# A transformer decoder in f32: the second feed-forward layer in 49 sub-products, with weight sums formed once and streamed

## The chip, the cores and the metric

The kernel runs on one core of a Trainium2 chip. Times are microseconds of device time for one execution. The core has a matrix engine (TensorE, PE in the profile; its weight loads are listed apart as PEld), VectorE (DVE), ScalarE (ACT), GpSimd (POOL), and SyncE (SP), from whose queue this kernel issues all of its DMA transfers. Every engine works through its own instructions in order. Matmul results go to PSUM, eight banks of 128 partitions x 512 f32 values; VectorE and ScalarE read them from there, and here GpSimd works on SBUF only. "Granted clock" is the share of full speed that TensorE's throttle allowed.

## The reference

An encoder layer over a short context (2 x 77 tokens), then a decoder layer over 2 x 2048 tokens of width 512, with 16 heads of width 32, all in f32. The change concerns the last step, the decoder's feed-forward:

```python
yn = _ln(y, dec_n1_s, dec_n1_b)
y = y + _mha(yn, yn, dec_sa_in_w, dec_sa_in_b, dec_sa_out_w, dec_sa_out_b, sb)     # causal
y = y + _mha(_ln(y, dec_n2_s, dec_n2_b), memory, dec_ca_in_w, dec_ca_in_b, dec_ca_out_w, dec_ca_out_b, cb)
h = _ln(y, dec_n3_s, dec_n3_b)
y = y + (jax.nn.relu(h @ dec_ff1_w.T + dec_ff1_b) @ dec_ff2_w.T + dec_ff2_b)       # 512 -> 2048 -> 512
```

## The kernel before

**Stages.** Tokens are handled in 8 blocks of 512 (`blocks`, four for each of the two sequences). First comes self-attention, in 128 *units* (block x 4 groups of heads x 4 token tiles of 128). A list of jobs is written out for every unit: `jobs` (projections), `light`, `ahead` and `late` (small work before and after them), run by `slot(n)`. The encoder is laid into the units of the first block, and the first block's cross-attention into the first units of the second sequence. The probabilities of two successive units lie at the two ends of one large buffer, `pp`; for a sequence's third block (units 32 to 47 and 96 to 111) they leave 4096 columns free in its middle, and parts of `vv` and `kT` are free then too.

**The feed-forward stage** follows, and with it the cross-attention of block x + 1 is interleaved with the feed-forward of block x. A block has 56 *slots*, 28 for each layer (L1100). In the last loop (L1350) a slot takes one step of `cross(x + 1)` and then `ff_slot`. `cross` (L1225) has a plan by slots: normalisation `n2` in slots 0 to 7, query projections in 9 to 12, and then for each token tile, seven slots apart from slot 14, score (+0), exp (+2), sums and normalisation (+3), transposes (+6), times V (+9), output product (+11) and the normalisation `n3` (+13, +15, +17). Cross-attention uses PSUM banks 0 to 3, the feed-forward 4 to 7.

**Two-by-two products.** Each of the two matrix products of the feed-forward is split into 2 x 2 quarters and done with seven products of quarters in place of eight (Strassen's scheme: `PARTS`, L1083, lists for each product the sum of left quarters, the sum of right quarters, and the result quarters to which it is added or from which it is taken). Layer 1: a product has four slots n of 4 matmuls, each with 128 x 128 weights and 256 tokens moving. Layer 2: likewise, with 128 x 128 pieces of h as weights and 256 output columns moving; the four slots of a product add up in PSUM. An f32 matmul is two records in the profile, a load and a multiplication each.

**Where the sums come from.** `prepare(s + 3)` (L1137) forms the operands of the slot three ahead, through L1148: sums of weight quarters and of n on GpSimd, sums of h quarters on VectorE. Both weight matrices lie in `pp` (`w_1`, `w_2`, loaded at L1053 and L1349), so that a sum of weights is formed anew in each of the 8 blocks. The results of every product are read out by themselves: in `first_product` ScalarE copies the first contribution to a quarter of h (L1178, L1176 with the sign turned), VectorE adds the later ones (L1180), and ScalarE applies the bias and relu after the last one (L1183). In `second_product` VectorE adds each result to the y in SBUF, at L1202, once or twice a product; y already holds the residual. Finished rows of y are stored at L1207, and the y of block x + 2 is loaded into the same place at L1209; two blocks of y are held.

**Queues.** All transfers stand in SP's one queue in program order, and a transfer that has to wait holds up those behind it. GpSimd's queue holds the sums of L1148, the row additions L750, the small powers L743 and the normalisation L804 of cross-attention.

Of the kernel before, what the change touches and what calls it, by code (L numbers as in the profile page):

```python
# [17 lines left out]
P = 128  # L18
B, T, S, D = 2, 2048, 77, 512
H, HD, DFF = 16, 32, 2048  # L20
NC = D // P
# [33 lines left out]
def tile_encoder_decoder(ctx: ExitStack, tc: tile.TileContext, ins, out):  # L55
# [102 lines left out]
    with (  # L158
# [751 lines left out]
        ahead = {n: [] for n in range(-1, len(units) + NU)}  # L910

# [83 lines left out]
        late = {n: [] for n in light}  # L995
# [21 lines left out]
        for r, fs in first_cross().items():  # L1017
# [3 lines left out]
        w_1 = pp[:, : END // 2].rearrange("p (c o) -> p c o", c=NC)  # L1021
        w_2 = pp[:, END // 2 :].rearrange("p (f o) -> p f o", f=NF)
        hT = kT.rearrange("p c (f n) -> p (c f) n", n=MB)
        vflat = vv.rearrange("p a d -> p (a d)")
        nT2 = vflat[:, 12 * D :].rearrange("p (c n) -> p c n", n=MB)
        pr = oT_all.rearrange("p a q -> p (a q)")[:, : H * S]
# [3 lines left out]
        ys = [  # L1030
            vflat[:, i * TB * D : (i + 1) * TB * D].rearrange("p (t d) -> p t d", t=TB) for i in range(2)
        ]

        first_ring = []

        def y_of(x, t):
            return ys[x % 2][:, t, :]
# [12 lines left out]

        def w_1_load(i):

            nc.sync.dma_start(w_1[:, :, ts(i, D)], wchunk("dec_ff1_wT", i * D))  # L1053
# [11 lines left out]
        def late_loads():  # L1065
# [12 lines left out]

        TOK = MB // 2
        PARTS = {  # L1083

            1: (((1, 1), "+", (2, 2)), ((1, 1), "+", (2, 2)), (("+", 1, 1), ("+", 2, 2))),
            2: (((2, 1), "+", (2, 2)), ((1, 1),), (("+", 2, 1), ("-", 2, 2))),
            3: (((1, 1),), ((1, 2), "-", (2, 2)), (("+", 1, 2), ("+", 2, 2))),
            4: (((2, 2),), ((2, 1), "-", (1, 1)), (("+", 1, 1), ("+", 2, 1))),
            5: (((1, 1), "+", (1, 2)), ((2, 2),), (("-", 1, 1), ("+", 1, 2))),
            6: (((2, 1), "-", (1, 1)), ((1, 1), "+", (1, 2)), (("+", 2, 2),)),  # L1090
            7: (((1, 2), "-", (2, 2)), ((2, 1), "+", (2, 2)), (("+", 1, 1),)),
        }
        ORDER = {1: (1, 4, 5, 7, 2, 3, 6), 2: (3, 5, 1, 4, 7, 2, 6)}

        def order_of(x, layer):

            return ORDER[layer if x else 2]

        SIGN = {"+": ALU.add, "-": ALU.subtract}
        slots = [  # L1100
            (x, layer, i, n)
            for x in range(len(blocks))
            for layer in (1, 2)
            for i in order_of(x, layer)
            for n in range(4)
        ]
        w_ring = [vflat[:, (8 + i) * D : (9 + i) * D].rearrange("p (c o) -> p c o", c=2) for i in range(4)]
        h_ring = [vflat[:, (12 + i) * D : (13 + i) * D].rearrange("p (c o) -> p c o", c=2) for i in range(4)]
        oflat = oT_all.rearrange("p a q -> p (a q)")
        n_ring = [  # L1110
            oflat[:, H * S + i * D : H * S + (i + 1) * D].rearrange("p (c o) -> p c o", c=2) for i in range(2)
        ]
        xt_ring = [pts_all[:, 7, :]]
        per = len(slots) // len(blocks)
        turns = {"w": 0, "h": 0, "n": 0, "xt": 0}
        operands, ff_banks = {}, {}

        def in_ring(name, ring):
            turns[name] += 1
            return ring[turns[name] % len(ring)]  # L1120

        def quarter_w1(a, c, n):
            o = (a - 1) * (DFF // 2) + n * 2 * P
            return w_1[:, 2 * c - 2 : 2 * c, o : o + 2 * P]

        def quarter_n(a, c, n):
            return nTt[:, 2 * a - 2 : 2 * a, ts(c - 1, TOK)]

        def quarter_h(a, c, n):
            f = (c - 1) * (NF // 2) + 2 * n  # L1130
            return hT[:, f : f + 2, ts(a - 1, TOK)]

        def quarter_w2(a, c, n):
            f = (a - 1) * (NF // 2) + 2 * n
            return w_2[:, f : f + 2, ts(c - 1, D // 2)]

        def prepare(s):  # L1137

            if s >= len(slots):
                return  # L1140
            x, layer, i, n = slots[s]
            early = s < 12

            def operand(parts, quarter, name, ring, engine):
                if len(parts) == 1:
                    return quarter(*parts[0], n)
                dst = in_ring(name, ring)
                engine.tensor_tensor(dst, quarter(*parts[0], n), quarter(*parts[2], n), SIGN[parts[1]])  # L1148
                return dst

            pa, pb, _ = PARTS[i]
            if layer == 1:
                b = operand(pb, quarter_n, "n", first_ring if early else n_ring, nc.gpsimd) if n == 0 else operands[s - 1][1]
                operands[s] = operand(pa, quarter_w1, "w", w_ring, nc.gpsimd), b
            else:
                b = operand(pb, quarter_w2, "w", w_ring, nc.gpsimd)
                operands[s] = operand(pa, quarter_h, "h", h_ring, nc.vector), b

        def first_product(s):
            x, layer, i, n = slots[s]  # L1160
            a, b = operands[s]
            mm = ff_bank()
            for f in range(2):
                for c in range(2):
                    nc.tensor.matmul(  # L1165
                        mm[:, ts(f, TOK)], a[:, c, ts(f, P)], b[:, c, :], start=(c == 0), stop=(c == 1)
                    )
            order = order_of(x, 1)
            got = mm.rearrange("p (f n) -> p f n", f=2)
            for sign, r, c in PARTS[i][2]:  # L1170
                users = [j for j in order if (r, c) in [u[1:] for u in PARTS[j][2]]]
                f = (r - 1) * (NF // 2) + 2 * n
                dst = hT[:, f : f + 2, ts(c - 1, TOK)]
                if i == users[0]:
                    if sign == "-":
                        nc.scalar.activation(dst, got, AF.Identity, scale=-1.0)  # L1176
                    else:
                        nc.scalar.copy(dst, got)  # L1178
                else:
                    nc.vector.tensor_tensor(dst, dst, got, SIGN[sign])  # L1180
                if i == users[-1]:
                    for e in range(2):
                        nc.scalar.activation(dst[:, e, :], dst[:, e, :], AF.Relu, bias=vec("dec_ff1_b", f + e))  # L1183

        def second_product(s):
            x, layer, i, n = slots[s]
            b, m = blocks[x]
            lhs, rhs = operands[s]
            if n == 0:
                ff_banks[x] = ff_pair()  # L1190
            mm = ff_banks[x]
            for c in range(2):
                for t in range(2):
                    nc.tensor.matmul(  # L1194
                        mm[:, t, :], lhs[:, c, ts(t, P)], rhs[:, c, :],
                        start=(n == 0 and c == 0), stop=(n == 3 and c == 1),
                    )
            if n < 3:
                return
# [194 lines left out]
```

## Time and profile before

| what | value |
|---|---|
| median of 3 runs (lowest to highest) | 2893.01 us (2889.47 to 2893.07) |
| the profiled execution: its time, its span | 2889.82 us, 2888.0 us |
| granted clock, mean | 0.992 |
| feed-forward stage, first matmul to end | 1756.8 to 2888.0 us |
| one block in that stage (the 2nd, 3rd, 5th, 6th and 7th) | 144.5 us |
| the 4th block, beside which the next sequence's bias tables are added | 148.4 us |
| the last block, without cross-attention | 101.3 us |
| PE idle in the 4th block; in each of the other later ones before the last | 3.1 us; below 0.1 us |
| DVE, ACT, POOL busy in a 144.5 us block | 90.6, 45.6, 83.8 us |
| DMA traffic over the span | 137 MB, 48 GB/s |
| DMA traffic from 1750 us on | 27 MB, 24 GB/s |

How to read it: the stage between 1756.8 us and the end is where the change works; an engine's busy time against the length of a block says how near it is to setting the pace. The busy share of PE counts a matmul from its start to its modelled end; the distance between starts is the pace.

### The profile page before, as it was taken

The page shows a single profiled execution, that of the slowest core. Times are in us where ns is not written, and L with a number is a line of the kernel's source. Part 1 is how long each engine was busy: PE and PEld are TensorE (multiplying, and loading weights), DVE is VectorE, ACT ScalarE, POOL GpSimd, SP SyncE. Part 2 cuts the span into 40 slices and gives each one's busy share as a digit, 9 for nine tenths or more (in the row PEclk, how much of TensorE's full clock was granted, in tenths as well). Part 3 has the DMA queues.
Part 4 walks back from the last instruction along what each step waited for, and adds up shares of the span by engine and source line. Part 5 has one row for each costly group of instructions (what it writes and reads, how often), then busy time and mean ns, then how long its engine had stood idle before and what let it go on. Part 6 is the DMA issues. An engine that isn't in the chain of part 4 may idle for free.

```text
span 2888.0 us, 60347 instructions
## 1 busy us (share of the span) xinstructions
PE 2852.6 (99%) x24438; PEld 2021.1 (70%) x24438; DVE 2048.3 (71%) x5566; ACT 1299.5 (45%) x2431; POOL 746.3 (26%) x605
## 2 busy tenths in 40 slices
PE   9899999999999999999999999999999999999999
PEld 5557666666666556666666677777777777777788
DVE  4667688878986678788778894757575757575745
ACT  3344465556665446565556674323232323232321
POOL 0100000000000101000000004465656474747464
PEclk9899999999999999999999999999999999999999
DMA  6413301201112502211201115000002000000000
GB/s 174 114 32 122 108 16 56 64 16 45 35 42 63 140 20 74 74 31 49 56 16 38 42 31 193 18 30 1 30 1 48 1 30 1 30 1 30 1 15 15
DMA packets 118456, 137.34 MB, mean 48 GB/s; under 512 B 18544, under 2 KB 73888, under 8 KB 118050
## 3 DMA queue, kind: packets, MB, share of 16 engines
q1 hardware_dynamic: 118178, 133.49, 16.0%
q8 instruction: 192, 3.15, 0.5%
q14 instruction: 86, 0.70, 0.1%
HBM read 111.59 MB, written 21.86 MB: 46 GB/s over the span
## 4 chain that ended last, share of the span: by engine, by line
PE 93%; DVE 4%; ACT 1%; DMA 1%; issue 1%; SPq 0%; POOL 0%; DVEq 0%; ACTq 0%; POOLq 0%
PE psum L425 17%; PE psum L1194 14%; PE psum L1165 13%; PE psum L371 11%; PE psum L442 8%; PE psum L830 4%; PE psum L765 4%; PE psum L239 4%; PE psum L251 4%; PE psum L215 4%; PE psum L226 3%; PE psum L810 2%; PE psum L780 1%; ACT pp L402 1%; PE psum L821 1%; PE psum L543 1%
## 5 line engine op out<-in xcount | busy, mean ns | idle before, releaser
L402 ACT ACTIVATE pp<-pp,nm 128x128 f32<-128x128 f32 (+15 forms) x512 | 611.6, 1201 | 267.1 <-DVE nm L397 266.8
L380 DVE TENSOR_SCALAR_CACHE_REDUCE pp<-psum 128x512 f32<-128x512 f32 (+3 forms) x1024 | 559.1, 590 | 58.1 <-PE psum L371 56.6
L425 PEld LDWEIGHTS psum<-ident,pp 128*128 128x128 f32 x4352 | 475.0, 142 | 110.2 <-DVE pp L380 51.6
L425 PE MATMUL psum<-ident,pp 128*128 128x128 f32 x4352 | 537.6, 278 | 8.3 <-DVE mx L387 3.7
L431 ACT COPY pts<-psum 128x512 f32<-128x512 f32 (+3 forms) x592 | 297.9, 575 | 473.2 <-PE psum L425 367.0
L1148 POOL TENSOR_TENSOR vv<-pp 128x512 f32<-128x512 f32 x320 | 418.9, 1325 | 154.1 <-PE psum L1165 133.5
L429 DVE COPY pts<-psum 128x512 f32<-128x512 f32 (+2 forms) x544 | 329.9, 659 | 67.3 <-PE psum L425 64.6
L371 PE MATMUL psum<-kT,q 32*128 32x512 f32 (+3 forms) x2560 | 362.4, 578 | 5.8 <-ACT pts L431 3.0
L442 PEld LDWEIGHTS psum<-pts,vv 128*32 128x32 f32 x8704 | 227.1, 110 | 125.2 <-issue 117.3
L442 PE MATMUL psum<-pts,vv 128*32 128x128 f32 x8704 | 280.5, 276 | 0.7 <-ACT pts L431 0.6
L1180 DVE TENSOR_TENSOR kT<-kT,psum 128x512 f32<-128x512 f32 x256 | 165.9, 680 | 113.2 <-PE psum L1165 104.9
L285 POOL TENSOR_TENSOR rstd<-rstd,mhalf 128x1 f32<-128x1 f32 x32 | 18.3, 571 | 875.2 <-DVE rstd L284 875.2
L371 PEld LDWEIGHTS psum<-kT,q 32*128 32x128 f32 x2560 | 125.6, 184 | 143.2 <-issue 88.6
L387 DVE CUSTOM_DVE_ANT_0 pp<-psum,bias 128x256 f32<-128x256 f32 (+1 forms) x512 | 195.8, 410 | 16.4 <-PE psum L371 16.4
L1183 ACT ACTIVATE kT<-kT,vecs 128x256 f32<-128x256 f32 x256 | 115.2, 499 | 176.0 <-DVE kT L1180 176.0
L1194 PE MATMUL psum<-vv 128*128 128x256 f32 x768 | 176.9, 381 | 0.0
L1165 PE MATMUL psum<-oT,vv 128*128 128x256 f32 x736 | 166.5, 380 | 0.0
L1194 PEld LDWEIGHTS psum<-vv 128*128 128x128 f32 x768 | 143.1, 190 | 26.8 <-issue 9.5
L1178 ACT COPY kT<-psum 128x512 f32<-128x512 f32 x124 | 69.6, 588 | 204.7 <-DVE kT L1180 134.2
L1165 PEld LDWEIGHTS psum<-oT,vv 128*128 128x128 f32 x736 | 138.8, 190 | 24.4 <-issue 6.2
L1148 DVE TENSOR_TENSOR vv<-kT 128x512 f32<-128x512 f32 x160 | 135.2, 859 | 13.4 <-PE psum L1194 12.4
L266 POOL TENSOR_TENSOR xr<-xr,row_dec_sa_out_b 128x512 f32<-128x512 f32 x30 | 38.4, 1282 | 373.8 <-DMA xr<-in_x_dram 212.6
(180 smaller groups left out, 3881.6 us busy)
## 6 DMA issues: line engine op xcount, KB each, us to landing
wqk<-in_dec_sa_in_wT_dram SPq DMA_DIRECT2D x64, 256.0 KB, 3.2
bias<-tzg SPq DMA_DIRECT2D x128, 128.0 KB, 3.9
wbig<-in_dec_sa_in_wT_dram SPq DMA_DIRECT2D x8, 1024.0 KB, 5.6
vv<-in_enc_ff_wT_dram SPq DMA_DIRECT2D x8, 1024.0 KB, 5.7
wbig<-in_dec_sa_out_wT_dram SPq DMA_DIRECT2D x8, 1024.0 KB, 5.7
vv<-y SPq DMA_DIRECT2D x32, 256.0 KB, 3.5
out_dram<-vv SPq DMA_DIRECT2D x32, 256.0 KB, 2.0
xt<-in_x_dram SPq DMA_DIRECT2D x30, 256.0 KB, 2.8
```

Source lines behind the costliest of these rows:

```text
L371: nc.tensor.matmul(banks[r][:, : kn * P], q[rows4(r), ts(t, P)], kT[rows4(r), g, k0 * P : (k0 + kn) * P], start=True, stop=True,)
L380: nc.vector.tensor_scalar(p[:, k0 * P : (k0 + far) * P], s[:, : far * P], 1.0, None, ALU.mult, ALU.max, accum_out=st["mx"][:, r, c : c + 1],)
L387: nc.vector.tensor_tensor_reduce(p[:, (i + 1) * P - w : (i + 1) * P], s[:, far * P : kn * P], biases[b, m, g][:, r, 2 * P - w :], 1.0, LOW ...
L402: nc.scalar.activation(p, p, AF.Exp, bias=nm, accum_out=to)
L425: nc.tensor.transpose(pt[:, ts(x, P)], state[n]["p"][r][:, ts(k, P)], ident)
L429: nc.vector.tensor_copy(pts[:, : len(load), :], pt[:, :w])
L431: nc.scalar.copy(pts[:, : len(load), :], pt[:, :w])
L442: nc.tensor.matmul(ot[rows4(r), t, :], vv[:, k, ts(g * HC + r, HD)], got.pop((n, k, r)), start=(k == 0), stop=(k == i),)
L1148: engine.tensor_tensor(dst, quarter(*parts[0], n), quarter(*parts[2], n), SIGN[parts[1]])
L1165: nc.tensor.matmul(mm[:, ts(f, TOK)], a[:, c, ts(f, P)], b[:, c, :], start=(c == 0), stop=(c == 1))
L1180: nc.vector.tensor_tensor(dst, dst, got, SIGN[sign])
L1194: nc.tensor.matmul(mm[:, t, :], lhs[:, c, ts(t, P)], rhs[:, c, :], start=(n == 0 and c == 0), stop=(n == 3 and c == 1),)
```

## The change

**Weight sums once.** During self-attention, in units 32, 34, 36 and 42 (`w2_sums`) and 96, 98, 100 and 106 (`w1_sums`), quarters of the two weight matrices are loaded into the free middle of `pp`, GpSimd forms all sums of them that will be needed, and they are stored to two DRAM tensors, `w1_d` (4 sums x 4 slots) and `w2_d` (7 products x 7 sub-products), each cut into tiles of 128 x 512. `w_1`, `w_2` and their loads are gone.

**Streaming.** In the feed-forward stage every weight operand is such a tile, of 256 KB. They are read in order of use into a ring of 16 tiles in the lower half of `pp`: 28 for layer 1 and 49 for layer 2 in every block. After a slot the ring is filled up again (`feed`); the first 16 are issued in the last unit but one of self-attention.

**Layer 2 in 49.** Each of its seven products is itself split into 2 x 2 quarters and done in seven sub-products of 4 matmuls with 128 columns moving, in four slots (2, 2, 2 and 1 sub-products). The sums of h now have two levels, `half_sum` and `sums_h`, formed four slots ahead, part on VectorE and part on GpSimd.

**Adding up in PSUM.** The scheme is another form of the seven products, with running sums: two chains, each on a pair of banks. A product of a chain is added to what the chain's banks already hold (`start` is set on its first only), so what is read out is the sum so far. In layer 1 a slot then has one read-out, in place of one or two. In layer 2 four small sums over both levels (`mixed`) are read out of PSUM by VectorE, and GpSimd adds the result to y.

**Also:** three blocks of y are held (a place freed by the operand rings); output rows are stored three slots after their last addition; the four sums of n are formed in a block's first slot (`sums_n`) by GpSimd; `nT2` and some scratch tiles have other places.

The core of what is added (what is taken out is `PARTS` to `ff_slot` of the listing above, `w_1`, `w_2`, and the first operands' `prepare`):

```diff
+        ON_W2 = {"11": 0, "21": 1, "22": 2, "T1": 3, "T2": 4, "T3": 5, "T4": 6, "12": 7}
+        SUBS = ("11", "21", "T2", "T1", "T3", "22", "T4")
...
+        def w2_sums(c):
+            src = ins["dec_ff2_wT"].rearrange("(r q c p) o -> r c p q o", r=2, q=2, p=P)
+            for r in range(2):
+                for o in range(2):
+                    z = tens[:, ON_W2[f"{r + 1}{o + 1}"]]
+                    nc.sync.dma_start(z, src[r, c][:, :, ts(o, TOK)])
+            z = {n: tens[:, i] for n, i in ON_W2.items()}
+            minus(gp, z["T1"], z["12"], z["11"])
+            minus(gp, z["T3"], z["22"], z["12"])
+            minus(gp, z["T2"], z["22"], z["T1"])
+            minus(gp, z["T4"], z["21"], z["T2"])
+            for (z0, z1), t in ones.items():
+                q = {f"{r + 1}{o + 1}": tens[:, z0:z1, r, ts(o, P)] for r in range(2) for o in range(2)}
+                t1, t2, t3, t4 = (t[:, k] for k in range(4))
+                minus(gp, t1, q["12"], q["11"])
+                minus(gp, t3, q["22"], q["12"])
+                minus(gp, t2, q["22"], t1)
+                minus(gp, t4, q["21"], t2)
...
+        def w1_store(n):
+            nc.sync.dma_start(
+                w1_d[:, n].rearrange("s p x -> p s x"), free[:, 4 * D :].rearrange("p (s x) -> p s x", s=4)
+            )
+        u = 2 * NU
+        for c, k in enumerate((0, 2, 4, 10)):
+            light[u + k + 2].append(lambda c=c: w2_store(c, 1))
+            late[u + k + 1].append(lambda c=c: w2_store(c, 0))
+        for c, k in enumerate((0, 2, 4, 10)):
+            light[u + k].append(lambda c=c: w2_sums(c))
+        u = 6 * NU
+        for n, k in enumerate((0, 2, 4, 10)):
+            light[u + k].append(lambda n=n: w1_sums(n))
+            late[u + k + 1].append(lambda n=n: w1_store(n))
...
+        ONE = (
+            ("11", "11", 0, True, "11"),
+            ("12", "21", 1, True, "11"),
+            ("S2", "T2", 0, False, "12"),
+            ("S1", "T1", 1, True, "22"),
+            ("S3", "T3", 0, False, "22"),
+            ("S4", "22", 1, False, "12"),
+            ("22", "T4", 0, False, "21"),
+        )
+        TWO = (
+            ("11", "11", 0, True, "11"),
+            ("S1", "T1", 1, True, "22"),
+            ("S2", "T2", 0, False, "12"),
+            ("S4", "22", 1, False, "12"),
+            ("S3", "T3", 0, False, "22"),
+            ("12", "21", 1, True, "11"),
+            ("22", "T4", 0, False, "21"),
+        )
+        first_slots = [(j, n) for half in range(2) for j in range(7) for n in (2 * half, 2 * half + 1)]
+        per = len(first_slots) + 4 * len(TWO)
+        FIRST = len(first_slots)
...
+        def weight_tiles():
+            for x in range(len(blocks)):
+                for j, n in first_slots:
+                    yield w1_tile(ONE[j][0], n)
+                for _, name, _, _, _ in TWO:
+                    for k in range(7):
+                        yield w2_d[ON_W2[name], k]
...
+        w_ring = [low[:, j % 4 * T + j // 4 * D : j % 4 * T + j // 4 * D + D] for j in range(16)]
+        tiles, fed, used = weight_tiles(), [0], [0]
+        def feed(upto):
+            while fed[0] < upto:
+                src = next(tiles, None)
+                if src is None:
+                    return
+                dst = w_ring[fed[0] % len(w_ring)]
+                fed[0] += 1
+                if len(src.shape) == 3:
+                    dst = dst.rearrange("p (c o) -> p c o", c=2)
+                nc.sync.dma_start(dst, src)
...
+        def sums_h(j, part):
+            name = TWO[j][0]
+            s = [by_f(s_ring[4 * (j % 2) + k]) for k in range(4)]
+            summed = name[0] == "S"
+            q = {k: of_h(name, k) for k in QUARTERS}
+            if part == 0:
+                if summed:
+                    half_sum(name, "21")
+                    half_sum(name, "22")
+                (gp if summed else ve).tensor_tensor(s[0], q["21"], q["22"], ALU.add)
+            elif part == 1:
+                if summed:
+                    half_sum(name, "11")
+                minus(gp, s[1], s[0], q["11"])
+            elif part == 2:
+                if summed:
+                    half_sum(name, "12")
+                minus(gp if summed else ve, s[2], q["11"], q["21"])
+            else:
+                minus(gp, s[3], q["12"], s[1])
+                lefts[j] = (q["11"], q["12"], s[1], s[0], s[2], s[3], q["22"])
...
+        pairs = ((6, 7), (4, 5))
+        turn_of = [0]
+        def start_turn():
+            p = turn_of[0] % 2
+            turn_of[0] += 1
+            return pairs[p], pairs[1 - p]
...
+            f = (int(to[0]) - 1) * (NF // 2) + 2 * f0
+            dst = hT[:, f : f + 2, ts(int(to[1]) - 1, TOK)]
+            if to == "21":
+                src = got
+            elif to not in [p[4] for p in ONE[:j]]:
+                nc.scalar.copy(dst, got)
+                return
+            else:
+                ve.tensor_tensor(dst, dst, got, ALU.add)
+                src = dst
+            for e in range(2):
+                nc.scalar.activation(dst[:, e, :], src[:, e, :], AF.Relu, bias=vec("dec_ff1_b", f + e))
...
+            i1, i2 = chains[0][chain]
+            for k in range(2 * part, min(2 * part + 2, 7)):
+                bank_i, col = ((i1, 0), (i1, 1), (i1, 2), (i2, 1), (i2, 2), (i2, 0), (i2, 3))[k]
+                lhs, w = lefts[j][k], next_w(4)
+                for c in range(4):
+                    nc.tensor.matmul(
+                        psum[:, bank_i, ts(col, P)], lhs[:, c, :], w[:, c, :],
+                        start=fresh and k in (0, 3) and c == 0, stop=c == 3, skip_group_check=True,
+                    )
+            one = psum[:, i1, :].rearrange("p (k n) -> p k n", n=P)
+            two = psum[:, i2, :].rearrange("p (k n) -> p k n", n=P)
+            c0 = 4 * (j % 2)
+            if part == 1:
+                nc.scalar.copy(mixed[:, 11], one[:, 0])
+                ve.tensor_tensor(
+                    mixed[:, c0 : 9 : 8 - c0], one[:, 1:3], mixed[:, 11:12].to_broadcast([P, 2, P]), ALU.add
+                )
+            if part < 3:
+                return
+            ve.tensor_tensor(mixed[:, 9:11], two[:, 1:3], mixed[:, 8:9].to_broadcast([P, 2, P]), ALU.add)
+            ve.tensor_tensor(mixed[:, c0 + 1 : c0 + 4 : 2], two[:, 0:2], mixed[:, 9:11], ALU.add)
+            ve.tensor_tensor(mixed[:, c0 + 2], two[:, 3], mixed[:, 10], ALU.add)
+            r, c = int(to[0]) - 1, int(to[1]) - 1
+            dst = ys[x % 3][:, 2 * r : 2 * r + 2, ts(c, TOK)]
+            gp.tensor_tensor(dst, dst, mixed[:, c0 : c0 + 4].rearrange("p (t o) n -> p t (o n)", t=2), ALU.add)
+            done = [t for t in ((0, 1) if j == 5 else (2, 3) if j == 6 else ())]
+            def store():
+                for t in done:
+                    nc.sync.dma_start(out_rows[b, m, :, t, :], y_of(x, t))
+            if x == len(blocks) - 1:
+                store()
+            elif done:
+                after[x * per + FIRST + 4 * j + 3 + 3] = store
...
+            k = n - FIRST + 4
+            if 0 <= k < 4 * len(TWO):
+                sums_h(k // 4, k % 4)
+            if n < FIRST:
+                first_product(n)
+            else:
+                second_product(x, (n - FIRST) // 4, (n - FIRST) % 4)
+            feed(used[0] + len(w_ring))
+            after.pop(s, lambda: None)()
+            if FIRST <= n < FIRST + TB:
+                new_y(x + 2, n - FIRST)
```

## The prediction

> **What bounds the kernel now.** I read the page's busy table and chain of waits first, then the busy times of chosen stretches, then single groups and places of the timeline.
>
> ```profile
> PE 2852.6 (99%) x24438; PEld 2021.1 (70%) x24438; DVE 2048.3 (71%) x5566; ACT 1299.5 (45%) x2431; POOL 746.3 (26%) x605
> ...
> PE 93%; DVE 4%; ACT 1%; DMA 1%; issue 1%; SPq 0%; POOL 0%; DVEq 0%; ACTq 0%; POOLq 0%
> ```
>
> TensorE is busy for 99% of the span and is 93% of the chain. In the feed-forward stage (from 1757 us) it is stricter still. The next stretches are a block's first layer, its second layer (both with the next block's cross-attention woven in), and the last block's second layer, which has none; columns: length, then busy time of PE, PEld, DVE, ACT, POOL, then clock, DMA share, GB/s.
>
> ```profile
> 2060.20:2135.70 75.50, 75.50 (x442) 58.32 (x440) 45.98 (x81) 32.59 (x70) 44.70 (x38) 1.00 0.05 15
> 2135.70:2204.70 69.00, 69.00 (x429) 55.40 (x426) 44.63 (x71) 13.04 (x27) 39.08 (x29) 1.00 0.05 16
> ...
> 2835.10:2888.00 52.90, 48.35 (x224) 42.21 (x223) 24.70 (x33) 0.91 (x2) 24.31 (x17) 0.98 0.06 20
> ```
>
> PE has no gap before the tail. Microseconds taken off PE here come off the end, as long as VectorE and GpSimd (45 and 39 us busy of 69) keep ahead.
>
> **TensorE's part.** Before, a block's second layer is 7 products x 4 slots x 4 = 112 matmuls of 256 columns, each two MATMUL records in f32: 224 records in 48.35 us, 0.216 us a record. After, it is 49 sub-products x 4 = 196 matmuls of 128 columns, 392 records. The first layer keeps its 112. So all hangs on the pace of a full 128x128 weight load with only 128 columns behind it. The kernel has that operation once, in the warm-up at line 982, whose last seven records run at the full clock; beside it the encoder's 154-column matmuls:
>
> ```profile
> 4.94 0.86 PEld L982 LDWEIGHTS psum<-ident 128*128 128x128 f32 x7
> 50.76 4.36 PE L543 MATMUL psum<-pp,vv 128*128 128x154 f32 x32
> ```
>
> Seven loads in 0.86 us, one of them lasting 0.192: (0.86 - 0.192) / 6 = 0.111 us a record; I take 0.1117, for the small step that the 154-column rows show at a change of bank. Those pace at (4.36 - 0.29) / 31 = 0.131, an upper bound, since they have more columns and equal weights; half of 0.216, 0.108, is the lower. Line 982 is the operation itself, so: 392 x 0.1117 = 43.8 us against 48.35, 4.57 less a block, **36.6 us less over eight**. The bounds: 0.108 gives 48 us less, 0.131 gives 24 us more.
>
> One rule speaks against the change: the Trainium skill, "TensorE: Matmul & The Clock Gate", section "Back-to-back issue gap", says that in a stream of load-and-multiply pairs narrow matmuls cost more than their columns, about 81 ns at 128 columns where columns alone would be 56. By that ratio a record here would take about 0.156 us (an estimate from that page), the second layer 61 us, and the kernel would be some 100 us slower. Line 982's 0.111 us contradicts it for f32, and the sum goes by the row.
>
> **VectorE and GpSimd.** Removed per block: 45 POOL sums at line 1148 (5 of n, 20 of each weight), 20 DVE sums of h, 20 of the 32 DVE adds at line 1180, the 12 at line 1202, one ACT copy in four. Added per block: 22 POOL and 22 DVE sums of h (4 and 4 for each of the four summed names, 2 and 2 for the three plain ones), 4 POOL sums of n, 7 POOL adds into y, 28 DVE read-outs of 128 or 256 columns. POOL goes from 45 to 33 operations, but 29 of them now fall into the second layer, next to DVE's own sums, and those two take turns:
>
> ```profile
> 2139.98 2.36 DVE L1148 TENSOR_TENSOR vv<-kT 128x512 f32<-128x512 f32 x2
> 2140.14 1.65 POOL L750 TENSOR_TENSOR vv<-vv,row_dec_sa_out_b 128x512 f32<-128x512 f32 x1 [4.02 <-DVE pts L749]
> ...
> 2143.90 0.63 DVE L1148 TENSOR_TENSOR vv<-kT 128x512 f32<-128x512 f32 x1
> ```
>
> A DVE sum takes 0.63 alone; here POOL's add takes 1.65 instead of 1.27, and the second DVE sum ends only after it. So I count both in one queue, 0.63 and 1.27. DVE operations that read PSUM are not held (line 1202 takes 0.68 to 0.69 beside POOL too).
>
> The narrow place is the sums for S1, S2, S4, S3, made one product early, in the layer's first 16 slots. Demand on the common queue: 16 x 0.63 + 16 x 1.27 + 3 adds into y x 1.27 = 34.2 us, and from the cross-attention two normalisations of about 2.25 (line 804), three row adds of 1.27 (line 750) and three centrings of 0.54 (line 749): 44.1 us. PE's time there: 16 slots at 4 x 6.25 = 25 us, plus two scores (1.06), two sets of transposes (1.74), two value products (1.01), two output products (3.43) and two n3 transposes (0.44): 15.4, so 40.4, and 8.4 more until the last sum is due in slot 46. Hence 44.1 against 48.8: on the whole it fits, narrowly. In single places it should not. DVE's queue, which I followed slot by slot with the durations above, runs some 4 us late after the 3.7 us of score read-outs in slot 28. The score in slot 35 needs the four PSUM banks that DVE still has to empty from slot 34 (about 1.1 us late), and the transpose in slot 38 waits for the centring behind the next read-outs (about 0.5 us). Queued behind PE there are the slot's own sub-products. I take **1.6 us a block, 11 us over seven**; the bounds are 0 and the 7.3 of the slower rival below.
>
> The last block has no cross-attention, so PE asks sooner: 34.2 us of sums against 25 + 4.5, **5 us** (bounds 0 and 7).
>
> **Sums formed once.** Units 32 to 42 get 16 loads, 48 POOL operations and 44 stores; units 96 to 106 get 8, 16 and 4. At 1.27 us that is 81 us of POOL, which is idle there (7 us busy between 385 and 615 us). Without that cover it would be 81 us on the path. DVE's work there reads PSUM, so it is not held. SP waits in its queue for POOL and for the stores before it may overwrite; behind it stand weight and bias loads. SP's issues now run about 0.75 to 2 slots of 10 to 17 us ahead of PE (the q2 weights are issued at 378 us and used at 432), while one round blocks SP some 10 to 25 us in pieces. I take **1 us**, bounds 0 and 15. The five loads of w_1 and w_2 that go were hidden.
>
> **The stream.** 77 tiles of 256 KB a block, 616 DMAs, each SP issue 0.3 to 0.5 us. 49 in 64 us take up to 25 us of SP and, with 0.084 us a packet of 2 KB, 49 x 128 x 0.084 / 16 = 33 us of the DMA engines. Loads of 256 KB land in 3.5 us; 16 tiles ahead are 14 us of PE. In the last block the need is (49 - 16) x 0.26 MB in 43.8 us, 198 GB/s, and the stretch from 4.9 to 5.7 us shows 302. I cost it at nothing; without that cover a late tile costs up to 3.5 us. Behind a tile that waits for PE in SP's queue stand only y loads due a block later and output stores, which are set three slots late. Product sums in PSUM alternate between two pairs of banks, so a read-out has a whole product of time: nothing.
>
> **The tail.** Before: one DVE add (0.69) and the store. After: a 128-column DVE add (0.3), a POOL add (1.27), the store: **1 us** more.
>
> **Sum.** -36.6 + 11 + 5 + 1 + 1 = -18.6. The profiled execution has a span of 2888.0 and a time of 2889.8, so 2871; the median shown is 3.2 us above that execution, so **2874** for the median. The likeliest case's own range is 2858 to 2887 (0.108 with small stalls; twice the stalls).
>
> **Rivals.** (1) *VectorE and GpSimd stay hidden everywhere.* For it: 4.7 us of slack, and POOL has 45 - 33 = 12 operations less. Against: 44.1 of 48.8 us leaves little. -36.6 + 2 = 2858. (2) *The common queue takes over from PE in every second layer, slower than before.* POOL also waits, in order, for DVE's reciprocals and variances: now 3.9 us before each of line 804 (110.3 us over 28) and 2.1 before each of line 743 (117.2 over 56). If these waits stay, 2 x 3.9 + 2 x 2.1 = 12 us join the 44.1: 56.1 against 48.8, 7.3 us a block, 51 in seven, and 5 in the last: -36.6 + 56 + 2 = +21, 2914. It decides from 4.2 us a block upwards. Against it: a late POOL no longer waits for DVE, as the work is there when it comes. (3) *128 columns pace at 0.131*, or the stream comes late by as much: then PE is slow enough to hide the sums, +24 + 2, 2919. (4) *The change doesn't do what it says*: the shorter product is eaten by waits at each of 49 new operands, 2893.
>
> **Chances.** Forecast 0.50, (1) 0.22, (2) 0.17, (3) 0.06, (4) 0.05. Faster by over 0.2% (5.8 us, about what a measurement of this kernel tells from no change): 0.47 + 0.22 + 0.03 of the rest = 0.72; within it 0.08; slower 0.20, from (2), (3) and a little of (4). The range goes from 2852, between (1) and its bound at 0.108, to 2908, most of the way to (2).
>
> **What would show it.** The 128-column records' pace in the last block (0.111, 44 us for 392); PE's idle time in second layers, and whether DVE or POOL ends it, in slots 35 and 38; POOL near 80% busy there; no PE wait on a weight tile; the stretch from 385 to 615 us as long as before. A pace above 0.123 or stalls above 4 us a block make the prediction wrong.

## The result, and the profile after

The kernel after takes 2882.53 us (median of 7 runs, 2880.44 to 2883.44), the one before 2889.96 us in the 7 runs made beside it (2886.28 to 2893.07): a ratio of **0.9973, 95% interval 0.9962 to 0.9985**, or 7.4 us less. The profiled executions have spans of 2888.0 and 2878.7 us, 9.3 us apart.

The page of the kernel after, busy times and the summary of the chain of waits:

```profile
PE 2827.8 (98%) x25782; PEld 2041.2 (71%) x25782; DVE 2033.3 (71%) x5550; ACT 1296.5 (45%) x2455; POOL 737.3 (26%) x573
...
PE 81%; DVE 8%; POOL 4%; ACT 3%; issue 3%; DMA 1%; SPq 0%; POOLq 0%; DVEq 0%; ACTq 0%
```

TensorE is busy for 24.8 us less (not for the 36.7 that its matmuls save, as part of a stall counts as busy: 65.59 us in the second layer below, where the same matmuls without stalls take 64.30 in experiment 3), and VectorE and GpSimd now hold 12% of the chain, where they had 4%. The next view lists TensorE's waits in the feed-forward stage by what it waited for (total us, times, longest). First the kernel before, then after:

```profile
PE psum L810 <- POOL oT L804: 1.5, 1, 1.5
PE psum L830 <- ACT xr L825: 0.9, 1, 0.9
PE psum L1165 <- DVE kT L1180: 0.8, 1, 0.8
```

```profile
PE psum L755 <- DVE xt L749: 6.5, 9, 1.1
PE psum L755 <- DVE pts L749: 3.0, 4, 1.1
PE psum L780 <- DVE pts L812: 2.3, 7, 0.3
PE psum L1332 <- POOL pp L1090: 1.6, 2, 1.2
PE psum L1332 <- DVE pp L1090: 0.3, 1, 0.3
```

Before, all three waits are in the 4th block. After, they are in every block, and most are for line 749, the centring ahead of a normalisation's transposes; no wait is for a weight tile. The stretches that answer to those of before are a block's first layer, its second, and the last block's second (length; busy PE, PEld, DVE, ACT, POOL; clock, DMA share, GB/s):

```profile
2057.80:2135.15 77.35, 76.15 (x442) 58.31 (x441) 36.45 (x65) 31.18 (x67) 21.27 (x18) 1.00 0.38 116
2135.15:2201.70 66.55, 65.59 (x596) 58.02 (x593) 52.21 (x85) 14.03 (x32) 52.57 (x35) 1.00 0.66 203
...
2825.61:2878.70 53.09, 44.98 (x393) 44.04 (x391) 29.61 (x45) 2.71 (x9) 39.52 (x27) 0.98 0.59 192
```

The second layer is 2.3 us shorter (68.89 to 66.56, from first matmul to first matmul), but **the first layer is longer, 77.34 against 75.65**, though its matmuls are the same and VectorE and GpSimd have less to do in it. The timeline of the kernel after shows why, at the beginning of a block (start, length, engine, line, operation; in brackets the idle time before it and what ended it):

```profile
2060.41 0.55 POOL L743 TENSOR_TENSOR crs<-crs,mhalf 128x1 f32<-128x1 f32 x1
...
2060.92 1.27 POOL L1090 TENSOR_TENSOR vv<-nT 128x512 f32<-128x512 f32 x1
...
2062.27 1.33 POOL L1090 TENSOR_TENSOR vv<-nT,vv 128x512 f32<-128x512 f32 x1
...
2063.56 1.27 POOL L1090 TENSOR_TENSOR vv<-nT 128x512 f32<-128x512 f32 x1
...
2064.79 1.27 POOL L1090 TENSOR_TENSOR vv<-nT,vv 128x512 f32<-128x512 f32 x1
...
2066.02 0.55 POOL L743 TENSOR_TENSOR crs<-crs,mhalf 128x1 f32<-128x1 f32 x1
...
2066.53 1.26 POOL L750 TENSOR_TENSOR vv<-vv,row_sa_bv 128x512 f32<-128x512 f32 x1
2066.60 1.48 DVE L749 TENSOR_SCALAR pts<-vv,cmv,crs 128x512 f32<-128x512 f32 x1 [2.51 <-POOL crs L743]
...
2068.14 0.66 PE L755 MATMUL psum<-ident,pts 128*128 128x128 f32 x4 [1.08 <-DVE pts L749]
```

The four sums of n now stand together in GpSimd's queue. Behind them waits the small power (L743) of the second token tile's normalisation; VectorE idles 2.51 us for it, then its centring takes 1.48 us beside a GpSimd row addition (0.54 alone), and TensorE stands still.

In the second layer the two places named in advance are there. Slot 35 first, then slot 38:

```profile
2147.39 5.18 DVE L1090 TENSOR_TENSOR pp<-pp,kT 128x512 f32<-128x512 f32 x3
2148.62 1.72 POOL L1090 TENSOR_TENSOR pp<-pp 128x512 f32<-128x512 f32 x1
...
2153.83 1.27 DVE L812 COPY pts<-psum 77x512 f32<-77x512 f32 x2
2154.56 0.45 PE L780 MATMUL psum<-pts,bias 32*128 32x77 f32 x4 [0.34 <-DVE pts L812]
...
2173.78 2.83 POOL L1351 TENSOR_TENSOR vv<-vv,oT 128x512 f32<-128x512 f32 x1
...
2176.58 1.71 POOL L1270 TENSOR_TENSOR pp<-pp 128x512 f32<-128x512 f32 x1
...
2178.26 0.54 POOL L743 TENSOR_TENSOR crs<-crs,mhalf 128x1 f32<-128x1 f32 x1
...
2178.84 1.48 DVE L749 TENSOR_SCALAR xt<-vv,cmv,crs 128x512 f32<-128x512 f32 x1 [1.67 <-POOL crs L743]
...
2180.37 0.65 PE L755 MATMUL psum<-ident,xt 128*128 128x128 f32 x4 [0.42 <-DVE xt L749]
```

In the first, three sums of h take VectorE 5.18 us beside GpSimd's (0.68 each alone), so its copies out of PSUM end late and the score waits. In the second, an add into y and a sum take GpSimd 4.5 us in place of 2.5, and power, centring and transposes are late in turn. The tail of the kernel after:

```profile
2871.40 1.06 PE L1332 MATMUL psum<-pp,kT 128*128 128x128 f32 x8
2872.49 0.42 DVE L1346 TENSOR_TENSOR oT<-psum,oT 128x256 f32<-128x256 f32 x1 [2.78 <-PE psum L1332]
...
2873.66 1.26 POOL L1351 TENSOR_TENSOR vv<-vv,oT 128x512 f32<-128x512 f32 x1 [4.99 <-DVE oT L1348]
```

Three read-outs in a row and a GpSimd add stand between the last matmul and the store. From the start of the last matmul to the end of the span it is 6.5 us, against 4.9.

### The profile page after: what moved, and what is told of

It reads as the page before. It is cut to its first block, busy times and chain, and to the rows that moved or that the text cites. A ratio compares the mean times of both kernels' runs of the same rounds, so it can differ in the third digit from the quotient of the medians.

```text
span 2878.7 us, 64333 instructions
## 1 busy us (share of the span) xinstructions
PE 2827.8 (98%) x25782; PEld 2041.2 (71%) x25782; DVE 2033.3 (71%) x5550; ACT 1296.5 (45%) x2455; POOL 737.3 (26%) x573
## 4 chain that ended last, share of the span: by engine, by line
PE 81%; DVE 8%; POOL 4%; ACT 3%; issue 3%; DMA 1%; SPq 0%; POOLq 0%; DVEq 0%; ACTq 0%
PE psum L425 17%; PE psum L371 11%; PE psum L1303 10%; PE psum L442 9%; PE psum L1332 7%; PE psum L765 4%; PE psum L215 4%; PE psum L239 4%; PE psum L251 4%; PE psum L226 3%; PE psum L830 3%; DVE pp L1090 2%; PE psum L780 1%; PE psum L810 1%; ACT pp L402 1%
## 5 line engine op out<-in xcount | busy, mean ns | idle before, releaser
L1332 PE MATMUL psum<-pp 128*128 128x128 f32 x2560 | 306.4, 276 | 1.9 <-POOL pp L1090 1.6
L1332 PEld LDWEIGHTS psum<-pp 128*128 128x128 f32 x2560 | 295.8, 192 | 17.4 <-issue 10.6
L1303 PE MATMUL psum<-vv,pp 128*128 128x256 f32 x1024 | 238.5, 381 | 0.0
L1303 PEld LDWEIGHTS psum<-vv,pp 128*128 128x128 f32 x1024 | 189.8, 190 | 32.2 <-issue 8.4
L1090 POOL TENSOR_TENSOR pp<-pp 128x512 f32<-128x512 f32 x124 | 171.6, 1399 | 105.2 <-DMA pp<-in_dec_ff_wT_dram 91.2
L1319 ACT ACTIVATE kT<-kT,vecs 128x256 f32<-128x256 f32 x192 | 87.7, 508 | 219.3 <-DVE kT L1316 219.2
L1303 PE MATMUL psum<-nT,pp 128*128 128x256 f32 x768 | 173.4, 379 | 0.0
L1303 PEld LDWEIGHTS psum<-nT,pp 128*128 128x128 f32 x768 | 145.3, 190 | 28.6 <-issue 10.2
L804 POOL TENSOR_TENSOR oT<-oT,cri 128x1232 f32<-128x1232 f32 x28 | 67.7, 2418 | 353.8 <-DVE cri L799 353.8
L1316 DVE TENSOR_TENSOR kT<-kT,psum 128x512 f32<-128x512 f32 x96 | 65.7, 686 | 119.1 <-PE psum L1303 89.7
```

The source lines that it names most:

```text
L1090: engine.tensor_tensor(out, a, b, ALU.subtract)
L1303: nc.tensor.matmul(mm[:, ts(f, TOK)], a[:, c, ts(f, P)], b[:, c, :], start=fresh and f == 0 and c == 0, stop=c == 1, skip_group_check=True,)
L1332: nc.tensor.matmul(psum[:, bank_i, ts(col, P)], lhs[:, c, :], w[:, c, :], start=fresh and k in (0, 3) and c == 0, stop=c == 3, skip_group_ ...
```

## The experiments

Blocks and layers are given from the start of a first matmul to that of the next layer's or block's. "Block" without more is the 3rd, 5th or 6th. One profile's span can be off by some 3 us for a reason outside the change: the feed-forward stage starts between 1754.4 and 1760.2 us in ten profiles, and the three kernels that share all code up to there (before and its two variants) start it at 1756.7, 1757.2 and 1760.2. The granted clock differs with it: between 625 and 670 us it was 1.00 in the profile that started earliest (experiment 6) and 0.92 in that of experiment 8, which started 4.7 us later. So layers are compared, and spans last.

**1. The sums of n, two at a time.**

```diff
-        def sums_n():
-            minus(gp, of_n("T1"), of_n("12"), of_n("11"))
-            minus(gp, of_n("T2"), of_n("22"), of_n("T1"))
-            minus(gp, of_n("T3"), of_n("22"), of_n("12"))
-            minus(gp, of_n("T4"), of_n("21"), of_n("T2"))
+        def sums_n(n):
+            if n == 0:
+                minus(gp, of_n("T1"), of_n("12"), of_n("11"))
+                minus(gp, of_n("T2"), of_n("22"), of_n("T1"))
+            if n == 5:
+                minus(gp, of_n("T3"), of_n("22"), of_n("12"))
+                minus(gp, of_n("T4"), of_n("21"), of_n("T2"))
...
-            if n == 0:
-                sums_n()
+            sums_n(n)
```

> The changed kernel, with the third and fourth sum of n moved from a block's slot 0 to its slot 5, behind the row additions; all is computed. In the changed kernel PE stands still 1.25 us before the n2 transposes of the second token tile in each of blocks 2 to 7 and 0.28 before the first query projection. Theory A: GpSimd's queue is the cause, since the four sums of n stand in it ahead of the small power that the second tile's centring needs. Then both waits go, 1.5 us a block in six blocks, some 9 us in all: ratio to the kernel before about 0.994. Rival: the centring is late because VectorE's queue is late (read-outs of the last product, statistics); then the wait stays above 0.8 us and the time is as that of the changed kernel (0.997).

Measured: 2871.27 us, ratio 0.9929 [0.9914, 0.9944]. The first layer is 75.65 us again, the second unchanged at 66.55, the block 142.20 in place of 143.89. Two sums ahead of the small power are harmless, four are not. The same place in this run:

```profile
2061.16 0.55 POOL L743 TENSOR_TENSOR crs<-crs,mhalf 128x1 f32<-128x1 f32 x1
...
2061.74 1.49 DVE L749 TENSOR_SCALAR pts<-vv,cmv,crs 128x512 f32<-128x512 f32 x1
```

The centring still takes 1.49 us beside a row addition, so its length is not the cause. Counted from the layer's start, the power comes at 5.74 us in place of 8.20, and that alone removes the loss: it is the order in GpSimd's queue.

**2. The copies of the transposed probabilities, all on ScalarE** in the feed-forward stage.

```diff
-                    if g % 2:
+                    if g % 2 and not copies:
                         nc.vector.tensor_copy
...
-                    bias_1 if biased and t else None,
+                    bias_1 if biased and t else None, True,
```

> The changed kernel, with VectorE's two copies per token tile out of the transposes' banks (L812) given to ScalarE in the feed-forward stage; all is computed. In slot 35 PE waits 0.8 us a block for banks that these copies empty. Theory A: VectorE's queue is late, and ScalarE (14 us busy of 66) is not; then the 0.8 us go and, with 1.2 us of VectorE's work less per tile, the later waits (0.2 before the transposes of the last tile, 0.6 before those of n3) shrink too: 0.8 to 1.6 us a block in seven blocks, 6 to 11 us in all, ratio to the kernel before about 0.994 to 0.995. Rival: what is late there is GpSimd, and the copies only show it; then the wait moves to the score's next reader and the time gains less than 2 us (0.997).

Measured: 2872.42 us, ratio 0.9934 [0.9917, 0.995]; second layer 65.24 us, first unchanged (77.32). The waits in slots 35 and 38 go, as Theory A said, and one grows, ahead of the last token tile's transposes, from 0.21 to 0.69 us. Slot 38 is relieved with slot 35, though GpSimd ended its wait: the add into y that took 2.83 us above takes 1.71 in this run. The timeline of this run:

```profile
2165.46 2.69 POOL L804 TENSOR_TENSOR oT<-oT,cri 128x1232 f32<-128x1232 f32 x1
...
2168.20 1.97 PE L810 MATMUL psum<-ident,oT 128*77 128x128 f32 x16 [0.52 <-POOL oT L804]
```

With TensorE earlier, GpSimd's normalisation, 2.69 us long where the shortest in this stage take 2.25, is the next to be late.

**3. GpSimd's second-level sums of h left out.** For S1 to S4, plain quarters are multiplied in place of these sums.

```diff
-                (gp if summed else ve).tensor_tensor(s[0], q["21"], q["22"], ALU.add)
+                if not summed:
+                    ve.tensor_tensor(s[0], q["21"], q["22"], ALU.add)
...
-                minus(gp, s[3], q["12"], s[1])
+                if summed:
+                    s = [q["22"], q["21"], q["11"], q["12"]]
+                else:
+                    minus(gp, s[3], q["12"], s[1])
```

> The changed kernel without GpSimd's four second-level sums of h for the products S1 to S4 in the second layer (other quarters of h stand in their place, so the result is another); VectorE's first-level sums and all matmuls stay. Theory A (the two engines take turns over sums whose operands lie in SBUF): VectorE's sums fall from about 1.4 to 0.65 us each, and the second layer loses all of its waits: 66.55 to about 64.9 us in a block with cross-attention, and the last block's second layer from 46.6 to about 44.1. Rival (VectorE has simply too many operations of its own): the wait for the banks in slot 35 stays at 0.5 us or more and the second layer at 66.0 or more; the last block's waits, which GpSimd ends, go in both.

Measured, in a single run: 2861.51 us, span 2859.7. A second layer, and the last block's:

```profile
1985.00:2049.30 64.30, 64.30 (x609) 56.84 (x608) 47.28 (x86) 15.88 (x36) 28.57 (x21) 1.00 0.64 197
...
2809.55:2853.20 43.65, 43.65 (x392) 43.64 (x391) 23.43 (x42) 2.71 (x9) 15.11 (x10) 1.00 0.68 222
```

TensorE is busy for all of both, and the rival is refuted. VectorE's own sums are all still there, yet it is busy for 47.28 us in place of 52.21: the 4.9 us are turns, time in which it waited for GpSimd's sums. 64.29 us is the second layer without stalls, 4.60 less than before, so the stalls of the kernel after cost 66.56 - 64.29 = 2.27 us a block, and in the last block 46.56 - 43.66 = 2.9. The run takes away the turns and GpSimd's own share of the sums together; how the stalls divide between the two it does not show.

**4. and 5. The 4th block of the kernel before**, which was 3.9 us longer than its neighbours (148.40 against 144.54). Its timeline:

```profile
2250.79 1.87 DVE L1180 TENSOR_TENSOR kT<-kT,psum 128x512 f32<-128x512 f32 x3
2251.50 1.71 ACT L1183 ACTIVATE kT<-kT,vecs 128x256 f32<-128x256 f32 x4 [7.08 <-DVE kT L1180]
...
2253.11 1.21 ACT L793 ACTIVATE oT<-oT 128x1232 f32<-128x1232 f32 x1
...
2258.52 1.97 PE L810 MATMUL psum<-ident,oT 128*77 128x128 f32 x16 [1.49 <-POOL oT L804]
```

The scores with a bias take VectorE longer (lines 787 to 790: one more operation of 0.48 us for each bank, and subtractions of 0.79 to 1.22 us in place of 0.48); its adds into h come late, ScalarE's exp waits behind relus that wait for these adds, and the transposes are late. First without GpSimd's sums of first-layer weights in this block (products of that block then use plain quarters), then without the later adds into h too:

```diff
-                if len(parts) == 1:
+                if len(parts) == 1 or x == 3 and layer == 1 and name == "w":
...
-                else:
+                elif x != 3:
```

> The kernel before, without GpSimd's sums of first-layer weights in the fourth block alone (the first quarter is used in place of the sum, so that part of the result is another). In the kernel before this block takes 148.4 us where the others take 144.5, and the changed kernel takes 143.9 in all. Theory A: VectorE's biased scores, which add two operands in SBUF, are slowed by GpSimd's sums (single subtractions of 0.8 to 1.2 us in place of 0.4 to 0.5), and the 3.6 us of PE's waits follow from that; without the sums the block takes 145.3 us or less. Rival: the wait comes from the loads of the bias tiles or from the mere number of additions; then the block stays at 147.5 us or more.

Measured, in a single run: 2888.93 us, the 4th block 147.0, between the two expectations; with the starts of TensorE's records set against those of run 5, delays of 1.28 and 1.18 us are left. GpSimd's weight sums were a third of it.

> The kernel before, in the fourth block's first layer without GpSimd's weight sums and also without VectorE's later additions of products into h (L1180), so that this part of the result is another. Without the weight sums alone the block took 147.0 us of 148.4, where the others take 144.5. Theory A: the rest comes from ScalarE's queue, in which the exponential stands behind relus that wait for those additions, which stand behind the biased scores in VectorE's; then the block takes 144.8 us or less. Rival: the biased scores are too long by themselves; then it stays at 146 or more.

Measured, in a single run: 2889.71 us, the 4th block 144.54, no wait left: Theory A holds. So the 3.9 us come from the 32 VectorE adds into h and GpSimd's weight sums beside the biased scores. The kernel after has 12 such adds and no weight sums in this layer, and its 4th block is as long as its neighbours (143.9 us).

**6. Four fixes in one:** 1 and 2; in the last block GpSimd's share of the sums for S1 to S4 on VectorE; and in the final product the bank's first two read-outs ahead of the last part, with the last add into y on VectorE.

```diff
+            gp = nc.vector if x == len(blocks) - 1 and TWO[j][0][0] == "S" else nc.gpsimd
...
+            final = x == len(blocks) - 1 and j == len(TWO) - 1
+            if part == (2 if final else 3):
+                ve.tensor_tensor(mixed[:, 9:11], two[:, 1:3], mixed[:, 8:9].to_broadcast([P, 2, P]), ALU.add)
+                ve.tensor_tensor(mixed[:, c0 + 1 : c0 + 4 : 2], two[:, 0:2], mixed[:, 9:11], ALU.add)
...
-            gp.tensor_tensor(dst, dst,
+            (ve if final else gp).tensor_tensor(dst, dst,
```

> The changed kernel with both edits before (sums of n late, copies on ScalarE) and two more: in the last block GpSimd's second-level sums of h for S1 to S4 go to VectorE, and at the end the last product's first two read-outs come before its last sub-product and its addition into y goes to VectorE. All is computed. Theory A (sums from SBUF of the two engines take turns, 0.63 on VectorE, 1.27 on GpSimd): in the last block the turns fall from 4 x 0.63 + 5 x 1.27 = 8.9 to 8 x 0.63 + 1.27 = 6.3 us a product against 6.25 of PE, so that its second layer falls from 46.6 to 44.0 us or less. Rival (VectorE cannot carry eight sums and its read-outs beside PE): it stays above 45.0. The tail after the last matmul, 6.5 us, falls to about 5.1. Blocks 2 to 7 at 140.9 us (both edits add up: 1.7 + 1.3 less). Span about 2855, ratio to the kernel before 0.988.

Measured: 2860.34 us, ratio 0.9891 [0.9878, 0.9905]. The first layer is 75.65 us, the second 65.25, the block 140.90 and the tail 5.1, all as expected, but the last block's second layer is 47.0, more than the 46.56 without this edit: there the rival holds. TensorE's waits in this stage, and the last block's second layer:

```profile
PE psum L810 <- POOL oT L804: 3.7, 7, 0.5
PE psum L1335 <- DVE oT L1350: 1.0, 1, 1.0
PE psum L1335 <- DVE pp L1090: 1.0, 2, 0.5
```

```profile
2803.30:2850.30 47.00, 44.83 (x392) 44.03 (x391) 34.56 (x60) 2.69 (x9) 15.23 (x10) 1.00 0.65 206
```

With all sums of S1 to S4 on VectorE, a product takes its queue 7.46 us where TensorE needs some 6.2 (43.66 / 7), though GpSimd stands idle for two thirds of the time. And the early read-outs (L1350) cost 1.0 us: the last part writes other columns of the same bank, and TensorE waited for the read-out to end.

**7. In all blocks, one sum of three (`s[2]`) on VectorE as well**, on top of 6.

```diff
-                minus(gp if summed else ve, s[2], q["11"], q["21"])
+                minus(ve, s[2], q["11"], q["21"])
```

> The kernel of c1, with one of GpSimd's four second-level sums (the third) given to VectorE in all blocks; all is computed. What is left in blocks with cross-attention is 0.7 us of PE's waiting for GpSimd's normalisation of the last token tile. Theory A: GpSimd's queue is late there by its own sums, and a sum moved to VectorE takes 0.63 of the common turns in place of 1.27; then the wait goes, 140.2 us a block, 5 us in all, ratio 0.986. Rival: VectorE, freed of the copies only, is late again; then PE waits for its read-outs or centrings, and the block is 140.9 or longer.

Measured: 2875.63 us, ratio 0.9945 [0.9931, 0.9958], 15 us worse than 6; second layer 67.24. Among the waits of this run:

```profile
PE psum L755 <- DVE xt L749: 4.3, 4, 1.1
PE psum L810 <- POOL oT L804: 3.7, 7, 0.5
PE psum L755 <- DVE pts L749: 3.2, 3, 1.1
PE psum L821 <- DVE oT L790: 2.9, 7, 0.4
```

The rival holds: the block is 142.88 us, the wait for GpSimd (L804) has not shrunk, and three new ones are for VectorE. A sum takes less time on VectorE, but it is in front of the read-outs and the centring there.

**8. The version built from what held:** 1 and 2; the last token tile's transposes one slot later; in the last block only `s[2]` on VectorE; the last add into y on VectorE, with the read-outs where they were.

```diff
-                for k, f in zip((0, 2, 3, 3, 6, 9, 11) if t else (-1, 1, 2, 3, 6, 9, 11), fs):
+                for k, f in zip((0, 2, 3, 3, 6 + t // 3, 9, 11) if t else (-1, 1, 2, 3, 6, 9, 11), fs):
...
-                minus(gp if summed else ve, s[2], q["11"], q["21"])
+                minus(gp if summed and x < len(blocks) - 1 else ve, s[2], q["11"], q["21"])
```

> All is computed. Against the run with four fixes: the transposes of the last token tile go one slot later, in the last block only the sum s[2] of S1 to S4 goes to VectorE, the final product's read-outs stay after its third part, and only its last add of y goes to VectorE. Theory (the 0.69 us wait is GpSimd's add being late by less than a slot; in the last block one sum of three is what VectorE can carry): no wait before the last tile's transposes, second layer 64.5 to 64.6 us, block 140.2 (140.9 before); last block's second layer 44.2 to 45, since GpSimd's turns drop from 8.9 to about 8.3 us per product; tail about 5.9; span about 2849, ratio to before 0.987. Rival (the place after is just as tight): the wait moves to the value products or the next score, blocks stay at 140.9; last block's second layer 46 or more; span 2854 to 2856, ratio 0.989.

Measured: **2856.61 us, ratio 0.9876 [0.986, 0.9893]**. The second layer is 64.79 us, the block 140.44, the last block's second layer 44.86, the tail 5.7. All of TensorE's waits in this stage that the list shows are one, in the last block:

```profile
PE psum L1334 <- DVE pp L1090: 0.5, 1, 0.5
```

```profile
2804.70:2849.70 45.00, 44.50 (x394) 44.05 (x392) 32.30 (x46) 2.71 (x9) 33.66 (x22) 1.00 0.68 216
```

The theory holds for both places by the layers, with 0.2 us a block left that it did not expect: against experiment 3, the n3 transposes of two token tiles come 0.24 and 0.29 us late. From its first to its last matmul the stage is 5.3 us shorter than in 6, where some 7 were expected. The profile's span, 2855.3, falls in the rival's range: the stage began 4.7 us later than in 6, in code that the two share. By the timed ratios alone, 8 and 6 overlap.

## Why the prediction was wrong

Its direction and its range held, but the gain was 9.3 us by the spans and 7.4 by the medians in place of 18.6. Term by term, from the profiles of the two kernels and experiment 3:

| term | predicted, us | measured, us |
|---|---|---|
| 392 records of 128 columns in place of 224 of 256 | -36.6 | -36.7 (7 x 4.60 + 4.47) |
| stalls in seven second layers | +11 | +15.9 (7 x 2.27) |
| stalls in the last second layer | +5 | +2.9 |
| first layers of blocks 2 to 7 | 0 | **+10.1** (6 x 1.69) |
| the 4th block's waits of before | 0 | **-3.9** |
| self-attention and sums formed once | +1 | +0.7, within the 3 us by which starts differ |
| tail | +1 | +1.6 |
| sum | -18.6 | -9.4 |

**The step that failed** is the one that looked for "the narrow place" only in "the layer's first 16 slots" of the second layer. The four sums of n were counted ("4 POOL sums of n") but never put into GpSimd's queue: their place was left at nothing without a reason, and the first layer has no term in the sum. A busy share of 21.27 us in 77.35 says nothing about the 5.1 us in which four sums stand in front of an operation that takes 0.55 us. Experiment 1 shows that this order is the whole of the 1.69 us a block: with it undone, the timed gain is 20.7 us (2891.93 to 2871.27), near the forecast's. That it comes so near is in part luck: the seven second layers stalled 4.9 us more than the sum had, while the last one, 2.1 less, and the 4th block, 3.9, made up for it.

Neither sign that the prediction had named for its failure appeared: the pace stayed under 0.123 us, and the stalls, 2.27 us in the second layer and 1.69 in the first, come to 3.96 a block, just under 4.

**TensorE's part** was right in mechanism and size: 392 records in 43.66 us without stalls are 0.111 us each. The rule that the prediction weighed against it (the Trainium skill, "TensorE: Matmul & The Clock Gate", section "Back-to-back issue gap") would have given some 61 us for the last block's second layer, by the prediction's estimate from that page; without stalls it took 43.66. The row of the warm-up, seven records long, was the better witness.

**The common queue** was right in kind. With the starts of TensorE's records set against those of experiment 3, slot 35 cost 1.36 us (1.1 predicted), by the copies named; slot 38 cost 0.64 (0.5), but not by a centring "behind the next read-outs": the centring waited for GpSimd's power, which stood behind an add into y. A third delay, ahead of the last tile's transposes (0.27), was not named; together 2.27 us a block in place of 1.6. What the prediction took at their length alone grew beside the other engine: centrings of 0.54 us to 1.48, normalisations of 2.25 to as much as 2.69. The last block was mis-sized: 5 us came from the difference of two sums, as though all the lateness fell into it, and 2.9 were measured.

**The 4th block** stood in the table of before with 3.1 us of idle TensorE, and the diff takes away 20 of its 32 VectorE adds and all of GpSimd's weight sums; the prediction did not ask what became of the idle time. Experiments 4 and 5 account for the 3.9 us.

**What held:** no wait for a weight tile; between 385 and 615 us TensorE's listed waits are the same as before (1.0 and 0.4 us, against 1.1 and 0.4), although GpSimd is busy for 48.93 us there in place of 7.13; GpSimd is busy for 79% of the second layer (52.57 of 66.55). Of the rivals, (1) is what experiment 8 comes near to when every order is mended (2856.61 against 2858, with the 4th block's 3.9 us in it), (3) is refuted by the pace, (2) fell, as even the longest second layer stayed shorter than before, and (4) too: the delays in a second layer stand at three places of the cross-attention, not at each new operand.

## What to carry to other kernels

When work is bundled into one place, put it into the queue of its engine and look at the next operation behind it that another engine needs soon; an engine's low busy share does not answer that. When a bound is lifted, list the places where the old kernel already waited, and ask of each whether it stays. And weigh moving a sum to another engine by who stands behind it there, not by its duration.

## What the runs showed of the hardware

- **Turns, and their size.** A centring from SBUF to SBUF takes VectorE 0.54 us alone and 1.48 beside a GpSimd addition; a sum 0.68 and 1.42; GpSimd's own sum 1.27 and 1.72; read-outs of 256 columns out of PSUM stay at 0.41 to 0.42. The Trainium skill, "SBUF — State Buffer", section "Who interferes with whom", says that VectorE's second pair of ports is shared with GpSimd, and that the instruction that comes first holds it to its end while the other waits in full. The first timeline agrees in the main: the centring that starts at 2066.60 ends at 2068.08, 0.29 us after the GpSimd addition that started at 2066.53 and took 1.26. That is less than the 0.54 it takes alone; which part of it does not wait, the row does not show.
- **A read-out in front of matmuls into other columns of its bank** held TensorE up by 1.0 us (experiment 6). The profile infers what ended a wait from semaphores, so this shows an order that the program keeps; whether the shared bank is the reason was not tried by itself.
- **Two records of 128 columns take about the time of one of 256** (2 x 0.111 and 0.216 us), though each has a full 128 x 128 weight load of its own.
